# VectorE's C product between the next slot's two scans, B products two slots ahead, column border at 384

## Chip, cores and metric

The kernel runs on one core of a Trainium2 chip. The metric is the time of one execution on the device in microseconds (us). The time before the change is the median of four runs.

## What is computed

Two residual blocks on x of shape (4, 512, 64, 64), float32: 4 batches, 512 channels, 4096 tokens.

```python
# layer 0: group norm, layer norm, a selective state-space model on each quarter of the channels
xn = layer_norm(tokens(group_norm(x)))
for each of 4 chunks of 128 channels:
    xi, z = split(chunk @ in_proj.T)               # 256 inner channels
    xc = silu(causal_conv4(xi) + conv_b)
    dt, Bs, Cs = split(xc @ x_proj.T)              # 8 + 16 + 16 columns
    dt = softplus(dt @ dt_proj.T + dt_b)
    # for every inner channel d and state s, over the tokens in order:
    h = exp(dt * A) * h + (dt * xc) * Bs
    y = sum_s(h * Cs) + xc * D
    chunk = (y * silu(z)) @ out_proj.T + skip * chunk
x = x + layer_norm(chunks) @ proj.T + proj_b
# layer 1: group norm, linear attention with relu on q and k, output projection, residual
x = x + attention(group_norm(x))
```

## The kernel before

The tokens of a batch are cut into tiles of T = 512. A **step** is one batch, one tile and one chunk of 128 channels: 4 x 8 x 4 = 128 steps. The recurrence over tokens is done by VectorE's scan instruction, which computes a * h + b along the 512 tokens for 128 partitions. A partition holds one pair of state and channel: 32 channels times 4 states. A step has 256 inner channels and 16 states, that is 32 scans, in 16 **slots** of two scans. In a step the slots go over e (two halves of the inner channels), q (four groups of four states) and jj (two pairs of channel blocks). Two slots, an even and an odd one, share one tile h and one C tile.

For slot g the engines do this:

- SyncE loads `b_all` (`b_row`): four rows of B, each spread over 32 partitions, for two slots at once, and `d_all` (`spread`): dt and dt * xc, twice a step. There are three buffers of `b_all` and two of `d_all`.
- GpSimd (POOL) makes the **B product** `bx` (`drive`, L467): 128 x 1024 elements. It is emitted one slot ahead, with two buffers.
- ScalarE (ACT) makes `dA` = exp(dt * A) into a PSUM bank (`decay`, L459), one for each scan, two scans ahead; there are two banks.
- VectorE (DVE) does the two scans (L484) and then the **C product** (L493), in place: h times C on the columns up to `CUT`, with C read from PSUM.
- The columns from `CUT` to 512 are the **border**: POOL multiplies them for both slots of a pair (L500) after the odd slot, with a copy of C that ScalarE makes (`c_copy`, L451). `CUT` is 512 - 160 = 352. Ahead of it POOL saves the last column of h as the state for the next tile (L499).
- TensorE (PE) spreads C over the partitions with a matmul (`c_row`, tile `c_all`, one PSUM bank) and sums h over the states into `y` (`fold_states`, 4 matmuls) after the odd slot.

All engines work through their queues in the order in which the program emits, which is written out by hand (`manual_schedule`). After the scans and the product of a slot `after()` emits the other work, by the slot number s in the step: at s = 1 the transfer of `d_all` for the second half, the `gate` product on POOL (L528) and the time-step matmuls; at s = 2 a table load, two softplus and another table load on ScalarE, and the output projection; at s = 3 the time-step product on POOL (L386) and its store; at s = 3 to 7 the input projection and convolution of a later step (`inputs`: matmuls `pc` and `pz`, copies `xz`, L359 and L368); at s = 9 another gate and `spread`; at s = 10 silu between two table loads, and the skip; from s = 11 the matmuls `pd` and the copies that make `dtr` and the parts of C (`mixers`).

The rest of the two layers lies in lists of pieces, `late` (layer norms, projection) and `rest` (attention). A credit of 3.2 matmuls a slot decides how many pieces a slot takes; slots 2 and 10 take none from there but one piece that may hold a long VectorE operation ("wide", 128 x 2048 elements).

The product and the C copy wait for each other in a chain: the even slot's product, the C copy, the odd slot's product.

Of the kernel before, what the change touches and what calls it, by code (L numbers as in the profile page):

```python
# [8 lines left out]
F32 = mybir.dt.float32  # L9
BF16 = mybir.dt.bfloat16  # L10
# [4 lines left out]
P = 128  # L15
T = 512
# [8 lines left out]
def kernel(  # L25
# [29 lines left out]
    NH = DI // P  # L55
    SUB = T // P
    LANE = 32
    CUT = T - 160
    BLK = 32
    KS = P // BLK  # L60
    NQ = NST // KS
# [59 lines left out]
        )  # L121
    sel = sel.rearrange("p q k i -> p q (k i)")

    minus = []
    for i in (2, 3):
        m = const.tile([P, P], BF16, tag=f"minus{i}", name=f"minus{i}")
        nc.vector.memset(m, 0.0)
        nc.vector.tensor_scalar(m[i * LANE :, :], ident[i * LANE :, :], -1.0, None, ALU.mult)
        minus.append(m)

    fold = const.tile([P, BLK], F32, tag="fold", name="fold")
    for k in range(KS):
# [19 lines left out]


    w_cv = const.tile([P, NTAP, DI], F32, tag="w_cv", name="w_cv")
    w_x = wk.tile([P, DI], F32, tag="bx", name="w_x", bufs=2)
    nc.scalar.dma_start(w_x, in_w[:, 0:DI])
    conv_bc = wk.tile([P, NTAP, DI], F32, tag="h", name="conv_bc", bufs=2)
    nc.scalar.dma_start(conv_bc, conv_w.partition_broadcast(P))
# [31 lines left out]
    w_qk = const_rows(wqk, "w_qk")  # L190

    bqk = const.tile([P, 2 * C], BF16, tag="bqk", name="bqk")
    b_all = wk.tile([P, 2 * C], F32, tag="bx", name="b_all", bufs=2)
    nc.scalar.dma_start(b_all, b_qkv[0 : 2 * C].partition_broadcast(P))
    bv = column(b_qkv[2 * C : 3 * C], NC, "bv")
    bo = column(b_out, NC, "bo")
# [177 lines left out]
            mm(f["pt"][e], w_dt[:, e * P : (e + 1) * P], f["dtr"][0:RANK, :], start=True, stop=True)  # L374

    def time_steps(f, nm):
        both = f["both"] = wk.tile([P, 2, NH, T], F32, tag="dt", name=f"dt_{nm}", bufs=1)
        for e in range(NH):
            nc.scalar.activation(
                both[:, 0, e, :], f["pt"][e], AF.Softplus, bias=dtb[:, e : e + 1]  # L380
            )

    def to_rows(f, v, nm):
# [16 lines left out]
    def mixers(f, nm):  # L400

        pd = work_bank(f"pd_{nm}")
        for e in range(NH):
            mm(pd, w_xp[:, e, :], f["xz"][:, 0, e, :], start=(e == 0), stop=(e == NH - 1))
        yield
        dtr = f["dtr"] = wk.tile([RANK + NST, T], F32, tag="dtr", name=f"dtr_{nm}", bufs=1)
        nc.scalar.copy(dtr, pd[0 : RANK + NST, :])
        b_rows = f["b_rows"] = dram.tile([NST, T], F32, tag="b_rows", name=f"b_rows_{nm}", bufs=3)  # L410
        nc.sync.dma_start(b_rows, dtr[RANK:, :])
        parts = f["parts"] = wk.tile([P, T], BF16, tag="parts", name=f"parts_{nm}", bufs=3)
        nc.scalar.copy(parts, pd)
        for i in (2, 3):
            yield
            mm(pd, minus[i - 2], parts, start=False, stop=True, skip_group_check=True)
            yield
            nc.scalar.copy(parts[i * LANE :, :], pd[i * LANE :, :])

# [1 line left out]

    JJ = NJ // 2
    SLOTS = NH * NQ * JJ

    def place(g):

# [36 lines left out]
    def drive(g):  # L463

        n, e, q, jj = place(g)
        bxs[g] = wk.tile([P, 2, T], F32, tag="bx", name=f"bx_{g}", bufs=2)
        nc.gpsimd.tensor_tensor(  # L467
            bxs[g], fs[n]["d_all", e][:, 1, jj * 2 : jj * 2 + 2, :], bc(b_all[g // JJ], 2), ALU.mult
        )

    def slot(g, last, in_scan, after):
        n, e, q, jj = place(g)
        b, t, c = steps[n]
        if jj and g + 5 < last:
            b_row(g + 5)
        if g + 1 < last:
            drive(g + 1)
        if jj == 0:
            hs[g // JJ] = wk.tile([P, NJ, T], F32, tag="h", name=f"h_{g}", bufs=2)
        h = hs[g // JJ]  # L480
        own = h[:, jj * 2 : jj * 2 + 2, :]
        for i in range(2):
            j = jj * 2 + i
            nc.vector.tensor_tensor_scan(  # L484
                h[:, j, :], dAs.pop(2 * g + i), bxs[g][:, i, :],
                0.0 if t == 0 else st[:, c, e, q, j : j + 1], ALU.mult, ALU.add,
            )
            if 2 * g + i + LEAD < 2 * last:
                decay(2 * g + i + LEAD)
        del bxs[g]  # L490
        in_scan()

        nc.vector.tensor_tensor(  # L493
            own[:, :, :CUT], own[:, :, :CUT], bc(c_all[g // JJ][:, :CUT], 2), ALU.mult
        )
        if jj == 0:
            c_copy(g)
        if jj == JJ - 1:
            nc.gpsimd.tensor_copy(st[:, c, e, q, :], h[:, :, T - 1])  # L499
            nc.gpsimd.tensor_tensor(  # L500
                h[:, :, CUT:], h[:, :, CUT:], bc(c_sb.pop(g // JJ), NJ), ALU.mult
            )
            if g + 1 < last:
                c_row(g + 1)
            fold_states(g)
        after()

    def fold_states(g):

# [243 lines left out]
    for g in range(0, 3 * JJ, JJ):  # L753
        b_row(g)
    c_row(0)
    drive(0)
    for k in range(LEAD):
        decay(k)

    with tc.manual_schedule():  # L760
        credit, mix = 0.0, iter(())
        for n, (b, t, c) in enumerate(steps):
            f, nm = fs[n], names[n]
            before = fs[n - 1] if n else None
            nxt = fs[n + 1] if n + 1 < N else None
            front = step_inputs(n + 2) if n + 2 < N else iter(())
            last_mix, mix = mix, mixers(fs[n + 2], names[n + 2]) if n + 2 < N else iter(())
            if c == 0 and (t + 1 < NT or b + 1 < B):
                add_to(late, tile_norm(b, t + 1) if t + 1 < NT else tile_norm(b + 1, 0))
            if c == 0 and t == 0 and b + 1 < B:  # L770
                add_to(light, input_norm(b + 1))
            if c == 2:
                while late and (b, t + 1) in xn and late[0][0].__name__ == "tile_norm":
                    one(late)
            for s in range(SLOTS):
                def in_scan():
                    if s == 0 and before is not None:
                        take_y(before, n - 1, 1)
                    if s == SLOTS // 2:
                        take_y(f, n, 0)  # L780

                def after():
                    nonlocal credit
                    start = work["mm"]
                    if s == 1:
                        spread(f, 1, nm)
                        if before is not None:
                            gate(before, 1)
                        if nxt is not None:
                            time_banks(nxt, names[n + 1])  # L790
                    if s == 2:
                        if nxt is not None:
                            nc.scalar.preload_act_table_set("softplus")
                            time_steps(nxt, names[n + 1])
                            nc.scalar.preload_act_table_set("natural_log_exp_and_others")
                        if before is not None:
                            out_proj(before, names[n - 1])
                    if s == 0:
                        next(last_mix, None)
                    if s == 10 and before is not None:  # L800
                        pb_, pt_, pc_ = steps[n - 1]
                        with_skip(before, xn[pb_, pt_], pc_)
                        if pc_ == NC - 1:
                            add_to(late, leave(pb_, pt_))
                    if s == 3:
# [12 lines left out]
                    if s >= 11:  # L818
                        next(mix, None)
                    if s in (2, 10):  # L820
                        if not (late and late[0][1] and one(late)):
                            one(light)
                        credit = 0.0
                        return
                    credit = min(credit + 3.2 - (work["mm"] - start), 3.2)
                    for queue in (late, rest):
                        if credit > 0:
                            start = work["mm"]
                            one(queue, wide=False)
                            credit -= work["mm"] - start  # L830

                slot(n * SLOTS + s, N * SLOTS, in_scan, after)
            fs[n - 1].clear() if n else None
    take_y(fs[N - 1], N - 1, 1)
    gate(fs[N - 1], 1)
    out_proj(fs[N - 1], names[N - 1])
# [57 lines left out]
```

## Time and profile before

| | |
|---|---|
| time, median of 4 runs | 8965.38 us (8948.59 to 8980.93) |
| profiled execution | 8961.52 us, span 8959.8 us |
| mean granted clock of TensorE | 0.863 |
| VectorE, GpSimd, TensorE, ScalarE busy | 7456.6, 7152.1, 6931.0, 5522.2 us |
| one scan; one C product; one B product; one border product; one dA | 1267, 888, 2359, 1541, 687 ns |
| first and last C product | 126.7 and 8465.7 us after the start |

The slots lie between these last two times; ahead of them the constants and the first statistics are made, and behind them the last batch's attention is finished. A line of the groups view gives the source line, the engine, the operation, the tiles it writes and reads with their shapes, the count, then the busy time in us with the mean duration of one in ns, then how long the engine sat idle before these instructions and what ended most of that. In the timeline the first column is the start in us, the second the duration of what was merged, and the bracket tells the idle time ahead and who ended it.

### The profile page before, as it was taken

Reading aid. Unit: us, or ns where it says so; the run is one execution under the profiler, and the core shown is the slowest. Engines: PE = TensorE matmul, PEld = TensorE weight load, DVE = VectorE, ACT = ScalarE, POOL = GpSimd, SP = SyncE. Lnnn points to the kernel's source line nnn. Section 1 sums busy time; section 2 is a strip of 40 time slices with the busy share of each in tenths; the row PEclk is TensorE's granted clock in tenths of the full one; section 3 lists DMA queues with packets and bytes.
Section 4 is the critical chain, followed back from the end, with each engine's and each line's share of the span. In section 5 each row is a group of like instructions: output and inputs, shape, how many; then the busy total and the mean of one; then the engine's idle time right before and its main releaser. Section 6 shows DMA issues by size and latency. Waiting matters only on the chain.

```text
span 8959.8 us, 80504 instructions
## 1 busy us (share of the span) xinstructions
PE 6931.0 (77%) x20885; PEld 2443.6 (27%) x20960; DVE 7456.6 (83%) x7097; ACT 5522.2 (62%) x8480; POOL 7152.1 (80%) x4565
## 2 busy tenths in 40 slices
PE   4667667677788877788788878778878887788799
PEld 1122222122223222232223222222222332222244
DVE  5998998888988888888888988888888888888700
ACT  4666666666666666666666666666666666666421
POOL 4988888888888888888888888888888888888600
PEclk8777787777889888899888989989888988989899
DMA  5555555555555555556554555556555555555502
GB/s 145 142 131 138 126 138 127 125 130 136 138 134 136 130 137 139 133 156 158 150 134 126 150 133 140 131 138 167 144 132 140 127 128 131 132 136 152 139 33 84
DMA packets 628274, 1197.31 MB, mean 134 GB/s; under 512 B 116056, under 2 KB 116576, under 8 KB 615520
## 3 DMA queue, kind: packets, MB, share of 16 engines
q1 hardware_dynamic: 620928, 1187.44, 51.8%
q10 hardware_dynamic: 6880, 4.70, 0.2%
q8 instruction: 164, 2.69, 0.1%
q14 instruction: 302, 2.47, 0.1%
HBM read 986.17 MB, written 205.52 MB: 133 GB/s over the span
## 4 chain that ended last, share of the span: by engine, by line
POOL 31%; PE 19%; issue 15%; DVE 15%; DMA 11%; ACT 5%; SPq 4%; POOLq 0%; DVEq 0%; ACTq 0%
POOL bx L467 23%; DVE h L484 12%; DMA d_all<-d_rows 7%; PE y L84 4%; PE pq L84 3%; PE pd L84 3%; PE pr L84 3%; POOL h L500 3%; POOL dt L386 2%; SPq L397 2%; PE pc L84 2%; DMA b_all<-b_rows 2%; POOL xz L528 2%; DVE h L493 2%; SPq L437 1%
## 5 line engine op out<-in xcount | busy, mean ns | idle before, releaser
L467 POOL TENSOR_TENSOR bx<-d_all,b_all 128x1024 f32<-128x1024 f32 x2048 | 4794.9, 2359 | 202.4 <-DVE h L484 184.9
L484 DVE TENSOR_TENSOR_SCAN h<-dA,st,bx 128x512 f32<-128x512 f32 x3584 | 4394.2, 1267 | 523.0 <-ACT dA L459 291.3
L459 ACT ACTIVATE dA<-d_all,a_t 128x512 f32<-128x512 f32 x4096 | 2771.3, 687 | 1781.4 <-DVE h L484 1770.5
L493 DVE TENSOR_TENSOR h<-h,c_all 128x704 f32<-128x704 f32 x2048 | 1818.9, 888 | 274.2 <-PE c_all L84 56.5
L84 PE MATMUL c_all<-parts,sel 128*128 128x512 bf16 x1024 | 448.0, 437 | 1592.0 <-DVE h L493 1589.2
L500 POOL TENSOR_TENSOR h<-h,c_sb 128x640 f32<-128x640 f32 x1024 | 1577.9, 1541 | 83.2 <-POOL st L499 1.8
L84 PE MATMUL y<-h,fold 128*32 128x512 f32 x8192 | 1360.8, 743 | 221.1 <-POOL h L500 218.5
L84 PE MATMUL pq<-w_qk,xa 128*128 128x512 f32 x2048 | 979.2, 611 | 6.3 <-issue 3.8
L84 PE MATMUL pc<-xn,w_cv 128*128 128x512 f32 x2048 | 946.1, 616 | 4.6 <-ACT xn L298 4.6
L499 POOL COPY st<-h 128x4 f32<-128x4 f32 x1024 | 191.8, 187 | 902.3 <-DVE h L484 862.2
L84 PEld LDWEIGHTS y<-h,fold 128*32 128x32 f32 x8192 | 175.4, 118 | 2172.2 <-POOL h L500 1880.3
L484 DVE TENSOR_TENSOR_SCAN h<-dA,bx 128x512 f32<-128x512 f32 x512 | 597.0, 1207 | 129.1 <-POOL bx L467 78.9
L84 PE MATMUL pr<-xb,m 128*128 128x512 f32 x1024 | 513.8, 645 | 66.8 <-DMA xb<-x 66.8
L84 PEld LDWEIGHTS pc<-xn,w_cv 128*128 128x128 f32 x2048 | 390.1, 196 | 582.8 <-issue 530.7
L84 PEld LDWEIGHTS pq<-w_qk,xa 128*128 128x128 f32 x2048 | 403.0, 198 | 448.1 <-issue 434.3
L84 PE MATMUL pp<-xn,w_pr 128*128 128x512 f32 x1024 | 484.6, 604 | 5.0 <-DVE xn L294 4.2
L451 ACT COPY c_sb<-c_all 128x160 f32<-128x160 f32 x1024 | 298.1, 291 | 260.8 <-DVE h L493 258.2
L359 ACT ACTIVATE xz<-pc,cb 128x512 f32<-128x512 f32 x256 | 175.9, 687 | 423.1 <-PE pc L84 389.0
L84 PE MATMUL pd<-xz,w_xp 128*128 128x512 f32 x512 | 395.9, 917 | 0.0
L84 PEld LDWEIGHTS <-sel 128*128 128x128 bf16 x1280 | 128.2, 100 | 973.6 <-DVE h L493 676.8
L561 DVE TENSOR_TENSOR kq<-pk,kq 128x512 f32<-128x512 f32 x124 | 85.1, 687 | 312.8 <-PE pk L84 312.5
L84 PE MATMUL y<-xz,dg 128*128 128x512 f32 x512 | 339.3, 752 | 0.0
(137 smaller groups left out, 7078.0 us busy)
## 6 DMA issues: line engine op xcount, KB each, us to landing
d_all<-d_rows SPq DMA_DIRECT2D x2048, 256.0 KB, 6.6
b_all<-b_rows SPq DMA_DIRECT2D x4096, 64.0 KB, 2.1
d_rows<-dt SPq DMA_DIRECT2D x256, 512.0 KB, 4.0
xs<-in_x_dram SPq DMA_DIRECT2D x32, 1024.0 KB, 11.3
xn<-in_x_dram SPq DMA_DIRECT2D x32, 1024.0 KB, 5.4
xr<-in_x_dram SPq DMA_DIRECT2D x32, 1024.0 KB, 5.4
x<-xr SPq DMA_DIRECT2D x32, 1024.0 KB, 3.9
xa<-x SPq DMA_DIRECT2D x32, 1024.0 KB, 5.4
```

The source lines that it names most:

```text
L84: nc.tensor.matmul(out_, lhsT, rhs, **how)
L359: nc.scalar.activation(xz[:, 0, e, :], pc[e], AF.Identity, bias=cb[:, e : e + 1])
L386: nc.gpsimd.tensor_tensor(f["both"][:, 1], f["both"][:, 0], f["xz"][:, 0], ALU.mult)
L397: nc.sync.dma_start(d[k * BLK : (k + 1) * BLK, v], src)
L451: nc.scalar.copy(got, c_all[g // JJ][:, CUT:])
L459: nc.scalar.activation(dAs[k], fs[n]["d_all", e][:, 0, j, :], AF.Exp, scale=a_t[:, e, j, q : q + 1])
L467: nc.gpsimd.tensor_tensor(bxs[g], fs[n]["d_all", e][:, 1, jj * 2 : jj * 2 + 2, :], bc(b_all[g // JJ], 2), ALU.mult)
L484: nc.vector.tensor_tensor_scan(h[:, j, :], dAs.pop(2 * g + i), bxs[g][:, i, :], 0.0 if t == 0 else st[:, c, e, q, j : j + 1], ALU.mult, AL ...
L493: nc.vector.tensor_tensor(own[:, :, :CUT], own[:, :, :CUT], bc(c_all[g // JJ][:, :CUT], 2), ALU.mult)
L499: nc.gpsimd.tensor_copy(st[:, c, e, q, :], h[:, :, T - 1])
L500: nc.gpsimd.tensor_tensor(h[:, :, CUT:], h[:, :, CUT:], bc(c_sb.pop(g // JJ), NJ), ALU.mult)
L528: nc.gpsimd.tensor_tensor(f["xz"][:, 1, e, :], f["xz"][:, 1, e, :], f["y", e], ALU.mult)
```

## The change

- The C product of slot g is emitted between the two scans of slot g + 1, with the C copy behind it and, for an odd slot, the next `c_row` and the fold. Slots 3 and 11 of a step (`BEHIND`) are the exception: their product comes after their own two scans. The border product stays at the end of the odd slot.
- `drive` is emitted two slots ahead, and `bx` has three buffers. `b_row` moves from odd slots (five ahead) to even slots (six ahead).
- `CUT` is 384 in place of 352: VectorE's product gets 2 x 384 elements a partition, POOL's border 4 x 128.
- What makes room for the third buffer: one matrix `minus` in place of two, and `dtr` as a part of the tile `dt` (`both`), which is now allocated in `mixers`.
- `take_y` moves from ahead of the product to the beginning of `after()`.

```diff
-    CUT = T - 160
+    CUT = T - T // 4
...
-        bxs[g] = wk.tile([P, 2, T], F32, tag="bx", name=f"bx_{g}", bufs=2)
+        bxs[g] = wk.tile([P, 2, T], F32, tag="bx", name=f"bx_{g}", bufs=3)
...
+    AWAY = (2, 10)
+    BEHIND = [s + 1 for s in AWAY]
...
-    def slot(g, last, in_scan, after):
+    def slot(g, last, after):
         n, e, q, jj = place(g)
         b, t, c = steps[n]
-        if jj and g + 5 < last:
-            b_row(g + 5)
-        if g + 1 < last:
-            drive(g + 1)
+        if g + 2 < last:
+            drive(g + 2)
         if jj == 0:
+            if g + 3 * JJ < last:
+                b_row(g + 3 * JJ)
             hs[g // JJ] = wk.tile([P, NJ, T], F32, tag="h", name=f"h_{g}", bufs=2)
...
             if 2 * g + i + LEAD < 2 * last:
                 decay(2 * g + i + LEAD)
+            if i == 0 and g and (g - 1) % SLOTS not in BEHIND:
+                product(g - 1, last)
         del bxs[g]
-        in_scan()
-
-        nc.vector.tensor_tensor(
-            own[:, :, :CUT], own[:, :, :CUT], bc(c_all[g // JJ][:, :CUT], 2), ALU.mult
-        )
-        if jj == 0:
-            c_copy(g)
         if jj == JJ - 1:
             nc.gpsimd.tensor_copy(st[:, c, e, q, :], h[:, :, T - 1])
             nc.gpsimd.tensor_tensor(
                 h[:, :, CUT:], h[:, :, CUT:], bc(c_sb.pop(g // JJ), NJ), ALU.mult
             )
+        if g % SLOTS in BEHIND:
+            product(g, last)
+        after()
+
+    def product(g, last):
+        _, _, _, jj = place(g)
+        own = hs[g // JJ][:, jj * 2 : jj * 2 + 2, :CUT]
+        nc.vector.tensor_tensor(own, own, bc(c_all[g // JJ][:, :CUT], 2), ALU.mult)
+        if jj == 0:
+            c_copy(g)
+        if jj == JJ - 1:
             if g + 1 < last:
                 c_row(g + 1)
             fold_states(g)
-        after()
...
-        dtr = f["dtr"] = wk.tile([RANK + NST, T], F32, tag="dtr", name=f"dtr_{nm}", bufs=1)
+        f["both"] = wk.tile([P, 2, NH, T], F32, tag="dt", name=f"dt_{nm}", bufs=1)
+        dtr = f["dtr"] = f["both"][0 : RANK + NST, 1, NH - 1, :]
...
-            mm(pd, minus[i - 2], parts, start=False, stop=True, skip_group_check=True)
+            mm(pd, minus, parts, start=False, stop=True, skip_group_check=True)
```

More of the change, by code (lines that the diff above doesn't have):

```diff
@@ L122 @@
     sel = sel.rearrange("p q k i -> p q (k i)")
[L124 to L129, printed above, removed]
+    minus = const.tile([P, P], BF16, tag="minus", name="minus")
+    nc.vector.memset(minus, 0.0)
+    nc.vector.tensor_scalar(minus[2 * LANE :, :], ident[2 * LANE :, :], -1.0, None, ALU.mult)
     fold = const.tile([P, BLK], F32, tag="fold", name="fold")
@@ L154 @@
     w_cv = const.tile([P, NTAP, DI], F32, tag="w_cv", name="w_cv")
-    w_x = wk.tile([P, DI], F32, tag="bx", name="w_x", bufs=2)
+    w_x = wk.tile([P, DI], F32, tag="bx", name="w_x", bufs=3)
     nc.scalar.dma_start(w_x, in_w[:, 0:DI])
@@ L192 @@
     bqk = const.tile([P, 2 * C], BF16, tag="bqk", name="bqk")
-    b_all = wk.tile([P, 2 * C], F32, tag="bx", name="b_all", bufs=2)
+    b_all = wk.tile([P, 2 * C], F32, tag="bx", name="b_all", bufs=3)
     nc.scalar.dma_start(b_all, b_qkv[0 : 2 * C].partition_broadcast(P))
@@ L376, in time_steps @@
     def time_steps(f, nm):
-        both = f["both"] = wk.tile([P, 2, NH, T], F32, tag="dt", name=f"dt_{nm}", bufs=1)
         for e in range(NH):
             nc.scalar.activation(
-                both[:, 0, e, :], f["pt"][e], AF.Softplus, bias=dtb[:, e : e + 1]
+                f["both"][:, 0, e, :], f["pt"][e], AF.Softplus, bias=dtb[:, e : e + 1]
             )
@@ L469, in drive @@
         )
-    def slot(g, last, in_scan, after):
+    def slot(g, last, after):
         n, e, q, jj = place(g)
         b, t, c = steps[n]
-        if jj and g + 5 < last:
-            b_row(g + 5)
-        if g + 1 < last:
-            drive(g + 1)
+        if g + 2 < last:
+            drive(g + 2)
         if jj == 0:
+            if g + 3 * JJ < last:
+                b_row(g + 3 * JJ)
             hs[g // JJ] = wk.tile([P, NJ, T], F32, tag="h", name=f"h_{g}", bufs=2)
         h = hs[g // JJ]
-        own = h[:, jj * 2 : jj * 2 + 2, :]
         for i in range(2):
@@ L755 @@
     c_row(0)
-    drive(0)
+    for g in range(2):
+        drive(g)
     for k in range(LEAD):
@@ L775, with after @@
             for s in range(SLOTS):
-                def in_scan():
+                def after():
+                    nonlocal credit
+                    start = work["mm"]
                     if s == 0 and before is not None:
@@ L780, in in_scan @@
                         take_y(f, n, 0)
-                def after():
-                    nonlocal credit
-                    start = work["mm"]
                     if s == 1:
@@ L819, in after @@
                         next(mix, None)
-                    if s in (2, 10):
+                    if s in AWAY:
                         if not (late and late[0][1] and one(late)):
@@ L830, in after @@
                             credit -= work["mm"] - start
-                slot(n * SLOTS + s, N * SLOTS, in_scan, after)
+                slot(n * SLOTS + s, N * SLOTS, after)
             fs[n - 1].clear() if n else None
+        product(N * SLOTS - 1, N * SLOTS)
     take_y(fs[N - 1], N - 1, 1)
```

## The prediction

> **What bounds the kernel now.** I read the page's busy shares and cost groups first, then the waits, then the timeline of one stretch in the middle. The groups show what a slot is made of and what its engines idle for:
>
> ```profile
> PE 6931.0 (77%) x20885; PEld 2443.6 (27%) x20960; DVE 7456.6 (83%) x7097; ACT 5522.2 (62%) x8480; POOL 7152.1 (80%) x4565
> ...
> L467 POOL TENSOR_TENSOR bx<-d_all,b_all 128x1024 f32<-128x1024 f32 x2048 | 4794.9, 2359 | 202.4 <-DVE h L484 184.9
> L484 DVE TENSOR_TENSOR_SCAN h<-dA,st,bx 128x512 f32<-128x512 f32 x3584 | 4394.2, 1267 | 523.0 <-ACT dA L459 291.3
> L459 ACT ACTIVATE dA<-d_all,a_t 128x512 f32<-128x512 f32 x4096 | 2771.3, 687 | 1781.4 <-DVE h L484 1770.5
> L493 DVE TENSOR_TENSOR h<-h,c_all 128x704 f32<-128x704 f32 x2048 | 1818.9, 888 | 274.2 <-PE c_all L84 56.5
> ...
> L500 POOL TENSOR_TENSOR h<-h,c_sb 128x640 f32<-128x640 f32 x1024 | 1577.9, 1541 | 83.2 <-POOL st L499 1.8
> ```
>
> No engine is full: DVE 83%, POOL 80%. There are 2048 slots in 128 steps of 16, some 65 us a step. DVE idles mostly in front of scans, and the waits view names two causes of about equal size:
>
> ```profile
> DVE h L484 <- ACT dA L459: 337.2, 256, 4.9
> ...
> DVE h L484 <- POOL bx L467: 278.3, 181, 46.5
> ...
> ACT c_sb L451 <- DVE h L493: 258.2, 649, 4.9
> ```
>
> (us in total, times, longest; 46.5 of the bx wait is the start of the kernel.) The change can take away the bx wait only; the dA wait comes from ScalarE, which stands in its queue behind table loads and behind copies that wait for TensorE. The third line: the C copy runs only after the product that reads the same C tile. The timeline of slots 2 to 5 of one step shows how these hang together:
>
> ```profile
> 4002.70 2.45 DVE L484 TENSOR_TENSOR_SCAN h<-dA,st,bx 128x512 f32<-128x512 f32 x2
> ...
> 4005.25 0.89 DVE L493 TENSOR_TENSOR h<-h,c_all 128x704 f32<-128x704 f32 x1
> ...
> 4006.23 0.29 ACT L451 COPY c_sb<-c_all 128x160 f32<-128x160 f32 x1 [0.35 <-DVE h L493]
> 4006.54 1.28 ACT L793 ACT_TABLE_LOAD   x1
> ...
> 4007.28 2.46 DVE L484 TENSOR_TENSOR_SCAN h<-dA,st,bx 128x512 f32<-128x512 f32 x2 [1.14 <-POOL bx L467]
> ...
> 4007.83 1.26 ACT L379 ACTIVATE dt<-pt,dtb 128x512 f32<-128x512 f32 x2
> ...
> 4010.07 1.53 POOL L500 TENSOR_TENSOR h<-h,c_sb 128x640 f32<-128x640 f32 x1
> ...
> 4011.19 2.46 DVE L484 TENSOR_TENSOR_SCAN h<-dA,st,bx 128x512 f32<-128x512 f32 x2 [0.46 <-PE c_all L84]
> 4011.57 2.35 POOL L386 TENSOR_TENSOR dt<-dt,xz 128x1024 f32<-128x1024 f32 x1
> ...
> 4013.89 4.65 POOL L467 TENSOR_TENSOR bx<-d_all,b_all 128x1024 f32<-128x1024 f32 x2
> ...
> 4016.27 2.46 DVE L484 TENSOR_TENSOR_SCAN h<-dA,st,bx 128x512 f32<-128x512 f32 x2 [1.63 <-POOL bx L467]
> 4016.45 0.69 ACT L359 ACTIVATE xz<-pc,cb 128x512 f32<-128x512 f32 x1 [1.43 <-PE pc L84]
> ```
>
> Slot 5's scans (4016.27) wait 1.63 us for a B product that POOL could begin only after the border product (L500) and the time-step product (L386). Slot 4's scans start when dA is ready, behind two table loads. And the copy at 4016.45 waits for TensorE's pc, which was queued behind the fold that waits for L500.
>
> **The change, part by part.** A step is 65.1 us; all sums are for one step, times 127.
>
> *The product between two scans.* Two scans in a row take 2.45 us although one takes 1.267: the second starts 0.08 before the first ends. The product starts 0.10 after the scan whose result it reads (4002.70 + 2.45 = 4005.15, then 4005.25). So that dependence costs 0.18 us. Between scans of another slot it should go: 14 of 16 slots (slots 3 and 11 keep the old place), 14 x 0.18 = 2.5 us. In the Trainium skill, "VectorE: DVE Perf Modes", section "The DRAIN you can't avoid", says that leaving out a semaphore between VectorE operations saves nothing, the next one waits for the pipe in any case; by that this term would be 0, and my forecast would rise by about 80 us to no change. The two intervals above, -0.08 and +0.10, disagree with it, and I go by them.
>
> *The border at 384.* Each VectorE product grows from 704 to 768 elements a partition. From 888 ns at 704 and 2280 ns at 2048 (L294) a further element costs 1.036 ns: +66 ns, 16 x 0.066 = +1.06 us. POOL's border product falls from 640 elements (1541 ns) to 512; the gate L528 of 512 elements takes 1274 ns: 8 x 0.267 = -2.1 us on POOL. The C copy on ScalarE falls from 0.29 to about 0.27.
>
> *B products two slots ahead.* The third buffer lets POOL write slot g+2's product as soon as slot g-1's scans are done, a slot (3.3 us) before it is needed in time. The 1.63 us of slot 5 and the like go, 278.3 - 46.5 = 232 us in all, 1.8 us a step. What is late next? In slot 4 dA, unchanged. In slots 6 and 7 dA again: in its queue stand the two copies of pc. I counted this over steps 2 to 125 of the timeline, from the end of slot 2's scans: slot 7's first dA ends at 18.9 us on average, and its scan starts at 19.4. So slot 7 already starts on ScalarE's word, and most of the bx wait is hidden by that. SP: the four b_row DMAs of a pair move from an odd slot, five ahead, to the even slot, six ahead; they and their reader both move by one, the lead stays four slots (14 us) against 2.1 us to landing. The d_all transfer is needed one slot (about 4 us) earlier; its last part is issued some 19 us before its first reader now and lands in 6.6 (longest 12.1). Both cost nothing; without that cover a B product would stall by what is missing.
>
> *What the later product does to others.* The product is emitted one scan later, and with it the C copy, the C broadcast and the fold. On ScalarE the C copy of slots 2 and 10 now stands behind the table loads and the dA of slots 4 and 12. Counted from the end of slot 2's scans: dA 0.74, load, two softplus and load 3.85 (1.28 + 1.26 + 1.28 and gaps), dA 0.69, copy 0.27: 5.6 us; behind silu likewise 0.74 + 1.28 + 1.91 + 1.28 + 0.69 + 0.27 = 6.2. The border product of slots 3 and 11 waits for it, and so does the odd product. It ends at 5.6 + 1.27 = 6.9 (7.1 now, on average) and 7.5 (7.5 now): the shorter border pays for the later start, no more. Behind it stand, on TensorE, fold and pc (slot 3) or fold and pd (slot 11), then ScalarE's copies, then slot 7's and slot 14's dA.
>
> So at slots 7 and 14 the scan starts at dA's time, and one product (0.87 us) is still to be done that is done by then now:
> - Slots 3 to 7: the fold follows the border at once in the new order (it starts 1.0 us after it now, TensorE being busy); I take half of that. dA at 18.4, slot 8 at 18.45 + 3.26 = 21.7, with the product 22.6, against 22.9 now: -0.3.
> - Slots 8 to 10: order gained and border paid, net 0.11 a slot: -0.2.
> - Slots 11 to 14: now the scan starts at 15.9 from the end of slot 10's scans, dA being ready at 15.1; new 15.3 + 0.87: +0.35.
> - Slots 14 to 2: four to five products at 0.11: -0.45.
>
> Sum -0.6 us a step, 127 x 0.6 = 76 us. The profiled execution took 8961.5 us (span 8959.8), the median of the runs is 3.9 above: 8885 and 8890.
>
> *Edits of no price.* One minus matrix instead of two (the second pass also subtracts in rows nobody reads): same matmuls, 0.2 us at the start. dtr inside the dt tile: its copy may wait for the d_rows DMAs of slot 3, nine slots earlier; without that cover it would wait the 4.0 us they take. take_y moves behind the product and waits for a fold emitted in its own slot; ScalarE has about 1.3 us to spare there, beyond that slot 2 or 10 waits for dA.
>
> **The rivals.**
> *All of it counts*: 2.5 - 1.06 + 1.8 = 3.2 us a step, 410 us: about 8560. For it: bx and the order are both on VectorE's path, and POOL has least to spare in steps without other work. Against: slot 7's dA follows at once. Chance 0.17.
> *TensorE late with C*: the broadcast and the fold now stand behind the work given out at the end of the slot before. From slot 3 to slot 6 TensorE does two pc groups (3.7 + 3.4 us), pz and perhaps two matmuls more, 0.9 to 2.6 us more than now before that broadcast. TensorE idles 1589 us in front of c_all now, which speaks against it. If the products of slots 6 and 14 wait 0.6 us a step together, nothing is left: 8960. Chance 0.13.
> *Slower*: the C copy behind the table loads delays border, fold, pc and pd, so that the dA of slots 7 and 14 comes no earlier than now. Then the uncovered product is paid in full at both, 2 x 0.87 = 1.74, less 0.65 from the order in the other slots: +1.1 us a step, 140 us: 9105. It decides from the point where the folds of slots 3 and 11 start no earlier than 8.1 and 7.6 us after the scans of slots 2 and 10, which are today's averages. For it: with nothing else on VectorE in slot 10 the border is 0.9 us later than today. Chance 0.27.
>
> **How the numbers follow.** My forecast has 0.43, with 8800 to 8950 of its own. What can be told from no change here is 0.3%, 27 us. Faster: 0.43 and 0.17, less a little: 0.59. Same: 0.13. Slower: 0.28. The range leaves out the ends of the first and third rival: 8640 to 9100.
>
> **What would show it.** Right: products start 0.08 before the scan ahead ends; bx waits under 60 us; dA waits above 337; border of slot 3 starting right after the C copy. The dA waits at slots 7 and 14 falling, or waits of products for c_all above 150 us, would prove the sum wrong.

## The result, and the profile after

| | before | after |
|---|---|---|
| time, median of 63 and of 42 runs | 8965.79 us | 8978.36 us (8962.81 to 8987.05) |
| profiled execution's span | 8959.8 us | 8976.8 us |
| mean granted clock of TensorE | 0.863 | 0.865 |

The ratio is 1.0012, interval 1.0008 to 1.0017: 0.12% slower, which is inside the bound of 0.3% named in the prediction. The forecast was 0.8% faster.

The page of the changed kernel, busy shares and cost groups (the columns as in the page before):

```profile
PE 6905.8 (77%) x20882; PEld 2443.7 (27%) x20960; DVE 7413.2 (83%) x7095; ACT 5422.8 (60%) x8480; POOL 6856.4 (76%) x4565
...
L482 DVE TENSOR_TENSOR_SCAN h<-dA,st,bx 128x512 f32<-128x512 f32 x3584 | 4469.4, 1270 | 496.9 <-issue 249.9
L466 POOL TENSOR_TENSOR bx<-d_all,b_all 128x1024 f32<-128x1024 f32 x2048 | 4790.8, 2359 | 99.8 <-DVE h L482 84.9
...
L505 DVE TENSOR_TENSOR h<-h,c_all 128x768 f32<-128x768 f32 x2048 | 1906.5, 931 | 359.7 <-ACT c_sb L450 235.3
...
L493 POOL TENSOR_TENSOR h<-h,c_sb 128x512 f32<-128x512 f32 x1024 | 1298.3, 1268 | 546.1 <-issue 223.8
...
L356 ACT ACTIVATE xz<-pc,cb 128x512 f32<-128x512 f32 x256 | 175.9, 687 | 529.4 <-PE pc L84 529.4
```

GpSimd got its room: 6856 us busy against 7152, and its B products idle 100 us where they idled 202. VectorE kept its idle time: 497 us ahead of these scans where it was 523, and 360 ahead of products where it was 274. New is what the products wait for: the C copy (`c_sb`). And ScalarE's `xz` copies wait 529 us for `pc` on TensorE, 389.0 before.

What VectorE gained and lost between its first scan and its last product can be added up from the two traces. A gap is the time from the end of one VectorE instruction to the start of the next; it is negative where the next one starts early. The gaps under 0.2 us ahead of products went from +209 to -122 us in all: so 331 us were gained. The larger products take 87 us more, and the gaps over 0.2 us, in which VectorE waits for another engine, grew from 741 to 983 us. With some 20 us more at the scans nothing is left.

The waits of the changed kernel (us in total, times, longest):

```profile
PE c_all L84 <- DVE h L505: 1697.6, 630, 15.6
PEld y L84 <- POOL h L493: 1363.0, 344, 8.6
...
ACT xz L356 <- PE pc L84: 529.4, 255, 4.9
...
DVE h L482 <- issue: 302.5, 198, 5.5
...
DVE h L505 <- ACT c_sb L450: 235.3, 139, 2.4
...
DVE h L482 <- ACT dA L458: 141.1, 106, 4.4
...
DVE h L505 <- PE c_all L84: 107.0, 46, 7.7
```

The scans' waits for `bx` fell from 278.3 to 54.0 us, of which 46.2 are the start of the kernel. The lines "issue" and "dA" of the scans have to be read with care, because a scan's wait is booked under the semaphore that came last by the profile. I went through every scan that started later than the instruction ahead of it allowed, and put the delay to whichever of its `dA` and `bx` had ended last. By slot, in us over the whole run (the last two rows are experiments, told below):

| | bx, slots 3 / 5 / 11 | dA, slot 4 | 6 | 7 | 12 | 14 |
|---|---|---|---|---|---|---|
| before | 39 / 177 / 20 | 114 | 42 | 45 | 37 | 123 |
| after | none | none | 220 | 126 | none | 193 |
| `e10_late_no_exception` | none | 108 | none | 86 | 80 | 26 |
| `e11_fold_behind` | 44 / 162 / 21 | 90 | none | 4 | 36 | 6 |

So the `bx` waits went, and the `dA` waits of slots 6, 7 and 14 took their place. Why `dA` is late there is seen in the timeline of slots 2 to 5 of one step of the changed kernel (start, duration, engine, idle time ahead and who ended it); slot 2's scans end at 3989.8:

```profile
3990.55 1.28 ACT L797 ACT_TABLE_LOAD   x1
3990.89 0.93 DVE L505 TENSOR_TENSOR h<-h,c_all 128x768 f32<-128x768 f32 x1
3991.74 1.28 DVE L482 TENSOR_TENSOR_SCAN h<-dA,st,bx 128x512 f32<-128x512 f32 x1
...
3995.05 0.26 ACT L450 COPY c_sb<-c_all 128x128 f32<-128x128 f32 x1
...
3995.34 0.95 DVE L505 TENSOR_TENSOR h<-h,c_all 128x768 f32<-128x768 f32 x1 [2.32 <-ACT c_sb L450]
3995.45 1.26 POOL L493 TENSOR_TENSOR h<-h,c_sb 128x512 f32<-128x512 f32 x1 [1.34 <-DMA d_all<-d_rows]
...
3996.35 0.38 PE L84 MATMUL c_all<-parts,sel 128*128 128x512 bf16 x1 [3.07 <-DVE h L505]
...
3996.77 1.22 PE L84 MATMUL y<-h,fold 128*32 128x512 f32 x8
3997.92 8.63 PE L84 MATMUL pc<-xn,w_cv 128*128 128x512 f32 x16
```

Slot 2's product is done at 3991.8, but its C copy comes only at 3995.05, behind the table loads. Slot 3's product, one of the two that stayed behind their own scans, waits 2.32 us for that copy with VectorE idle. The border reads the copy too and starts 0.14 us behind it (the bracket names a DMA, the one that landed last by the profile). On TensorE the broadcast of the next C (`c_all`) waits 3.07 us for slot 3's product, the fold behind it for the border, and `pc` stands behind both: it starts 8.1 us after slot 2's scans.

Over steps 2 to 125 a step takes 65.33 us, before 65.35: in the middle of the kernel nothing changed. The 17 us between the two profiled executions lie at the ends. The first scan starts 3.4 us later, steps 0 and 1 (up to the end of slot 2's scans in step 2) take 7.2 more, the 120 us from the end of slot 2's scans in step 126 to the end of the last product contain 11.8 more (there three products wait 4.88, 5.39 and 3.92 us for `c_all`, where the longest such wait before was 1.38), and 124 steps together with the tail give 5.3 back.

### The profile page after: what moved, and what is told of

It is laid out like the page before. It is cut to its first block, busy times and chain, and to the rows that moved or that the text cites. A ratio compares the mean times of both kernels' runs of the same rounds, so it can differ in the third digit from the quotient of the medians.

```text
span 8976.8 us, 80691 instructions
## 1 busy us (share of the span) xinstructions
PE 6905.8 (77%) x20882; PEld 2443.7 (27%) x20960; DVE 7413.2 (83%) x7095; ACT 5422.8 (60%) x8480; POOL 6856.4 (76%) x4565
## 5 line engine op out<-in xcount | busy, mean ns | idle before, releaser
L482 DVE TENSOR_TENSOR_SCAN h<-dA,st,bx 128x512 f32<-128x512 f32 x3584 | 4469.4, 1270 | 496.9 <-issue 249.9
L458 ACT ACTIVATE dA<-d_all,a_t 128x512 f32<-128x512 f32 x4096 | 2815.4, 689 | 1938.6 <-DVE h L482 1917.2
L505 DVE TENSOR_TENSOR h<-h,c_all 128x768 f32<-128x768 f32 x2048 | 1906.5, 931 | 359.7 <-ACT c_sb L450 235.3
L493 POOL TENSOR_TENSOR h<-h,c_sb 128x512 f32<-128x512 f32 x1024 | 1298.3, 1268 | 546.1 <-issue 223.8
L84 PE MATMUL pt<-dt,w_dt 8*128 8x512 f32 x512 | 350.4, 815 | 4.0 <-ACT dt L406 2.7
```

Of the source, the lines that this page charges most:

```text
L84: nc.tensor.matmul(out_, lhsT, rhs, **how)
L458: nc.scalar.activation(dAs[k], fs[n]["d_all", e][:, 0, j, :], AF.Exp, scale=a_t[:, e, j, q : q + 1])
L482: nc.vector.tensor_tensor_scan(h[:, j, :], dAs.pop(2 * g + i), bxs[g][:, i, :], 0.0 if t == 0 else st[:, c, e, q, j : j + 1], ALU.mult, AL ...
L493: nc.gpsimd.tensor_tensor(h[:, :, CUT:], h[:, :, CUT:], bc(c_sb.pop(g // JJ), NJ), ALU.mult)
L505: nc.vector.tensor_tensor(own, own, bc(c_all[g // JJ][:, :CUT], 2), ALU.mult)
```

## Experiments

All ratios are against runs of the kernel before that were taken together with those of the experiment; their medians lie between 8966 and 8974 us, so differences of less than 10 us between two experiments mean little. At first three theories stood against one another for the lost gain: the late C copy of slots 2 and 10; the `dA` waits that take the place of the `bx` waits, whatever the copy does; and TensorE coming late with the broadcast of C. Later runs tested a fourth, the exception itself, that is the slots 3 and 11 in which the product, the `c_row` and the fold stay ahead of the other work.

### The parts alone

**The border alone** (`e4_cut_only`): before, with one line changed.

```diff
-    CUT = T - 160
+    CUT = T - T // 4
```

> The kernel before with the border at 384. VectorE's product grows by some 43 ns (931 against 888 ns as measured in the changed kernel), 88 us in all; POOL's border falls from 1541 to 1268 ns, which brings the B products of slots 3, 5 and 11 forward by 0.27 us, some 50 to 80 us. All theories: 8940 to 9010 us; this prices the border alone.

8951.35 us, 0.9976 (0.9967 to 0.9984): a gain of 21 us, and not a loss, though VectorE is the busiest engine.

```profile
L493 DVE TENSOR_TENSOR h<-h,c_all 128x768 f32<-128x768 f32 x2048 | 1955.4, 955 | 272.7 <-PE c_all L84 55.2
```

The C product takes 955 ns here, 67 more than the 888 of before. The 931 ns of the changed kernel, from which the expectation took its 43, hold a second thing: at its later place a product is shorter by some 25 ns whatever the border (888 ns at the old place and 861 in `e13_late_352` with the border at 352; 955 and 929 in `e10_late_no_exception` with 384). So 2 x 67 ns of VectorE were worth less here than GpSimd's 270 ns a border. TensorE's granted clock was higher as well (0.872 in the median of these runs, 0.861 in those of the kernel before), and its share of the 21 us isn't known.

**B products two slots ahead, alone** (`e2_ahead_only`): before, with the three buffers and what makes room for them.

```diff
-        if jj and g + 5 < last:
-            b_row(g + 5)
-        if g + 1 < last:
-            drive(g + 1)
+        if g + 2 < last:
+            drive(g + 2)
...
+            if g + 3 * JJ < last:
+                b_row(g + 3 * JJ)
```

> The kernel before, with nothing but the B products two slots ahead in three buffers (and the room for it: one minus matrix, dtr inside dt, b_row at even slots); product order and border at 352 stay. Both theories: the bx wait falls from 278 to about 50 us. Copy theory: the C copy keeps its early place, so most of the 232 us are gained: 8760 to 8850 us. dA theory: the waits turn into dA waits of slots 6 and 7 one for one: 8930 to 8965 us.

8934.75 us, 0.9956 (0.9943 to 0.9970): a gain of 37 us of the 232 that the scans' waits for `bx` amounted to. The waits turned into `dA` waits: by the same count as above 161 us in slot 4, 118 in slot 6, 99 in slot 7, 122 in slot 14.

**The later product alone** (`e3_order_only`): the changed kernel with `drive` one slot ahead, two buffers and the border at 352.

> The changed kernel with B products one slot ahead in two buffers again and the border at 352: the product's place is all that is left. The order saves 0.18 us in 14 slots of a step. Copy theory: border and odd product wait for the late C copy, the B product of slot 5 comes still later behind the border, so the bx wait rises above 350 us and the time to 9000 to 9100 us. dA theory: the product that is still open when dA comes late costs about what the order saves: 8940 to 8990 us.

9404.56 us, 1.0483 (1.0469 to 1.0497), far beyond both expectations. The waits view of this kernel tells why:

```profile
DVE h L482 <- POOL bx L466: 1078.0, 710, 48.3
```

With two buffers the B product of slot g + 1 can start when the scans of slot g - 1 are done, and is needed by the first scan of slot g + 1. Between them VectorE used to do product, scan, scan, product, about 4.3 us. In the new order it does scan, product, scan, about 3.3 us. Behind an odd slot GpSimd needs 1.55 + 0.19 + 2.36 = 4.1 us for border, state and B product. The waits for `bx` indeed lie in the odd slots alone, 63 to 403 us in each. So the later product needs the third buffer: the two parts are not independent, and their prices alone don't add up.

**B products ahead and border, product at its old place** (`e9_no_order`): `e2_ahead_only` with `CUT` at 384.

> B products two slots ahead and the border at 384, with the product directly behind its own two scans as before (the C copy then stands ahead of the table loads by itself). Copy theory with the parts adding: e2 (8935) less what the border alone gave (21): about 8910, so the product's new place is worth 130 us once the C copy is early. If the product's place is worth its full 0.18 us in 14 slots (320 us): 9100 would be needed, which nothing supports. If it is worth nothing: 8780.

8910.71 us, 0.9934 (0.9920 to 0.9949), as expected. With two of the three parts the kernel is 55 us faster than before; with the third it is 13 us slower.

### The C copy

**Late copy in the kernel before** (`e6_copy_late`): the C copy of slots 2 and 10 moves behind the table loads, all else stays.

```diff
+            if i == 0 and (g - 1) % SLOTS in (2, 10):
+                c_copy(g - 1)
...
-        if jj == 0:
+        if jj == 0 and g % SLOTS not in (2, 10):
             c_copy(g)
```

> The kernel before, with one thing changed: the C copy of slots 2 and 10 is emitted in the next slot behind its first scan and dA, and so behind the table loads, where the change has put it. Copy theory: the border products of slots 3 and 11 and the odd product wait for the copy as in the changed kernel (products wait some 200 us for it), the B product of slot 5 comes later behind the border: 100 to 250 us slower than before, 9070 to 9220 us. dA theory: within 40 us of before.

9126.34 us, 1.0176 (1.0158 to 1.0193). The late copy by itself costs 160 us, 1.3 a step.

**Early copy in the changed kernel** (`e1_copy_first`): the C copy of slots 2 and 10 is emitted right after their scans, ahead of the table loads.

```diff
+        if g % SLOTS in AWAY:
+            c_copy(g)
...
-        if jj == 0:
+        if jj == 0 and g % SLOTS not in AWAY:
             c_copy(g)
```

> The changed kernel, with the C copy of slots 2 and 10 emitted right after the slot's scans, ahead of the table loads, and the product of these slots after it. Copy theory (the C copy behind the table loads holds the border product, the odd product, and so the fold and pc or pd, and gives the gains back): products no longer wait for the C copy (235 us now), the border product of slot 3 starts 1 to 2 us earlier where no long VectorE operation stands in slot 2, dA waits of slots 6, 7 and 14 shrink; 8750 to 8880 us against 8978. dA theory (ScalarE's queue and TensorE's pc and pd set the dA of slots 6, 7 and 14 whatever the C copy does): dA waits there stay above 450 us in all, and the time within 30 us of 8978. TensorE theory (broadcast and fold come late behind the work handed out before): no change either, and products still wait for c_all over 100 us.

8779.49 us, 0.9785 (0.9772 to 0.9798): the late copy costs the changed kernel 199 us. But the `dA` waits did not go away: 145, 126 and 190 us in slots 6, 7 and 14. The products wait 89 us for `c_all`, under the 100 that the TensorE theory needed.

**The `xz` copies one slot later** (`e7_xz_later`): `e1_copy_first`, with the four copies of `pc` and `pz` to `xz` emitted a slot later, so that `dA` doesn't stand behind a copy that waits for TensorE.

> The changed kernel with the early C copy (8779 us), and the four copies xz emitted one slot later than now, so that each comes two slots behind its matmuls. dA theory, in the part that is left to it: the dA waits of slots 6 and 7 (270 us together in that kernel) are ScalarE waiting for pc ahead of dA; they fall below 80 us, the wait of xz for pc from 452 to under 100 us, and the time by 60 to 200 us, to 8580 to 8720. If the dA is late for another reason (VectorE itself frees the bank late), the waits stay and the time is within 30 us of 8779.

8760.16 us, 0.9768 (0.9752 to 0.9784). The `dA` waits of slots 6 and 7 fell from 270 to 40 us, but the time fell by 19 us only, against 60 to 200 expected: from slot 2 to slot 8 a step is 0.97 us shorter, from slot 8 to slot 10 it is 0.76 longer, and the products' waits for `c_all` rose from 89 to 224 us. So the order of ScalarE's queue is not what costs the time. That `pc` comes late on TensorE is what is left, and the next experiments test it.

### The exception

**No exception, early copy** (`e8_no_exception`) and **no exception, late copy** (`e10_late_no_exception`): one line of `e1_copy_first` and the same line of the changed kernel.

```diff
-    BEHIND = [s + 1 for s in AWAY]
+    BEHIND = []
```

> The changed kernel with the early C copy, and slots 3 and 11 no longer excepted: all products between the next slot's scans. The broadcast and fold of slot 3 then stand behind pc on TensorE. dA theory: pc no longer waits for the border and the fold, so the dA waits of slots 6 and 7 fall below 150 us (270 now); against it the products of slots 4 and 5 wait for c_all. TensorE theory: those waits are larger, over 200 us: 8800 to 8950 us. If the first weighs more: 8650 to 8750.

> The changed kernel with one thing altered: slots 3 and 11 are no longer excepted; the C copy of slots 2 and 10 stays late, behind the table loads. If the exception cost what it did with the early copy (8779 to 8442, 337 us) and the late copy costs its 199 us besides: 8640. If the late copy hurts only through the exception (there the odd product follows at once and waits for it, and the fold and pc behind that): 8440 to 8500, and products wait for the C copy less than 60 us.

8441.88 us, 0.9410 (0.9394 to 0.9426), and 8404.14 us, 0.9364 (0.9351 to 0.9377). Both are below everything that was expected (8650 and 8440 at the lowest). So that one line costs the changed kernel 574 us, and without it the late copy does no harm: the kernel with it is 38 us the faster. The page and the waits of `e10_late_no_exception`:

```profile
PE 6784.8 (81%) x20882; PEld 2422.0 (29%) x20960; DVE 7380.5 (88%) x7095; ACT 5418.7 (64%) x8480; POOL 6848.0 (82%) x4565
```

```profile
PE c_all L84 <- DVE h L505: 908.7, 500, 15.9
PEld y L84 <- POOL h L493: 678.9, 352, 6.4
...
DVE h L482 <- ACT dA L458: 155.2, 120, 4.2
...
DVE h L505 <- PE c_all L84: 109.0, 43, 8.0
ACT xz L356 <- PE pc L84: 93.3, 85, 3.4
...
```

The work is the same, the shares rise. TensorE waits 909 us for a product ahead of the broadcast of C where it waited 1698 in the changed kernel, its folds wait 679 us for a border where they waited 1363, and ScalarE's `xz` copies wait 93 us for `pc` where they waited 529. The same slots in the timeline of this kernel; slot 2's scans end at 3732.8:

```profile
3736.44 3.60 PE L84 MATMUL pc<-xn,w_cv 128*128 128x512 f32 x8
3738.09 0.26 ACT L450 COPY c_sb<-c_all 128x128 f32<-128x128 f32 x1
3738.24 1.28 DVE L482 TENSOR_TENSOR_SCAN h<-dA,st,bx 128x512 f32<-128x512 f32 x1 [2.18 <-issue]
3738.49 1.27 POOL L493 TENSOR_TENSOR h<-h,c_sb 128x512 f32<-128x512 f32 x1 [1.39 <-ACT c_sb L450]
3739.44 0.93 DVE L505 TENSOR_TENSOR h<-h,c_all 128x768 f32<-128x768 f32 x1
...
3740.73 1.06 PE L84 MATMUL y<-h,fold 128*32 128x512 f32 x8
3741.73 3.70 PE L84 MATMUL pc<-xn,w_cv 128*128 128x512 f32 x8
```

The C copy is as late as in the changed kernel, 5.3 us after slot 2's scans. But slot 3's product is now done in slot 4, when the copy is there, and the first `pc` group runs at 3.6 us, ahead of the broadcast and the fold, while TensorE would otherwise wait for the product and the border. On average over steps 2 to 125 the first `pc` matmul starts 4.8 us after slot 2's scans, 8.6 in the changed kernel, and the first `pd` matmul 4.1 us after slot 10's, 9.7 in the changed kernel.

The mean time from mark to mark over steps 2 to 125, in us, cuts the step into four parts. "s8" is the start of slot 8's first scan, "2 end" the end of slot 2's scans; where one product is still to be done at a mark, 0.85 has been added to the part before it and taken from the part behind:

| | 2 end to s8 | s8 to 10 end | 10 end to s14 | s14 to 2 end | step |
|---|---|---|---|---|---|
| before | 22.88 | 9.69 | 15.87 | 16.92 | 65.35 |
| after | 22.66 | 9.55 | 16.59 | 16.52 | 65.33 |
| `e10_late_no_exception` | 20.39 | 9.55 | 14.29 | 16.54 | 60.77 |

The exception costs 2.27 and 2.30 us a step, in the parts that hold slots 3 and 11, and nothing in the two others. How much of it is the product that waits for the copy, and how much the place of the broadcast and of the fold, was not tried in the changed kernel one by one.

**The fold behind the other work, in the kernel before** (`e11_fold_behind`): the products stay at their old place; in slots 3 and 11 only the other work is emitted ahead of `c_row` and the fold, so that `pc` and `pd` stand before them in TensorE's queue.

```diff
+            if g % SLOTS in (3, 11):
+                after()
             if g + 1 < last:
                 c_row(g + 1)
             fold_states(g)
+            if g % SLOTS in (3, 11):
+                return
         after()
```

> The kernel before, with one thing moved: in slots 3 and 11 the broadcast of the next C and the fold are emitted behind the work of the slot, so that on TensorE pc and pd stand ahead of them. Queue-order theory (pc and pd wait in TensorE's queue behind a fold that waits for POOL's border): the dA wait of slot 14 (about 129 us) goes nearly, that of slots 6 and 7 shrinks, the B product of slot 5 still comes late behind the border (175 us stay): 8800 to 8900 us against 8966. If the fold's place does not matter: 8940 to 8990. If the broadcast coming later holds the products: over 9000 us, and products wait for c_all above 150 us.

8858.47 us, 0.9872 (0.9858 to 0.9885). The `dA` waits of slots 6, 7 and 14 all but vanish (table above), while the `bx` wait of slot 5 stays. The products wait more for the broadcast, which comes later: 56.5 us before, 215 now, without the loss that the last expectation tied to it.

```profile
DVE h L484 <- POOL bx L467: 257.1, 174, 46.9
...
DVE h L493 <- PE c_all L84: 215.4, 169, 6.6
```

**The same with B products ahead and the border at 384** (`e14_ahead_fold_behind`): `e9_no_order` with the edit of `e11_fold_behind`.

> B products two slots ahead and the border at 384 with the product directly behind its own scans (8911 us), and in slots 3 and 11 the broadcast and the fold behind the work of the slot. What is left against the changed kernel without the exception (8404) is the product's place. If the place is worth its 0.18 us in all 16 slots, 127 x 2.9 = 366 us: about 8770. If most of the gain is the fold's place and the B products' lead: 8450 to 8600. If the products wait for c_all in slots 4 and 12 as they did with the fold behind in the kernel before (215 us): about 8900.

8789.10 us, 0.9795 (0.9782 to 0.9809). Against `e9_no_order` the place of the broadcast and the fold is worth 122 us; against `e10_late_no_exception`, in which the products also lie between the next slot's scans, 385 us are left. That is 385 / (127 x 16) = 0.19 us a product. The profiled executions, 416 us apart (411 of them between the first scan and the last product), show what it is made of, by the same count of gaps as for the changed kernel: 361 us are short gaps ahead of products, 0.18 us each. The shorter products (52 us) and the waits over 0.2 us (503 against 460) add 95, and the scans take 47 back.

### A faster version

With the fold out of the way, VectorE and not GpSimd should set the time, so I put the border back to 352, in `e8_no_exception` (`e12_border_352`) and in `e10_late_no_exception` (`e13_late_352`).

> The fastest kernel so far (early C copy, no exception, 8442 us) with the border back at 352. VectorE is 88% busy there, GpSimd 81%. If VectorE sets the time: 43 ns less in 2048 products, 60 to 90 us faster, 8350 to 8385. If GpSimd's longer border (273 ns in 1024 products) delays the B products or the fold: 8440 to 8520, and the scans wait for bx above 80 us.

> The changed kernel without the exception (8404 us), with the border at 352. VectorE's products are 43 ns shorter, GpSimd's border 273 ns longer. If VectorE sets the time as with the early C copy, where this gave 45 us: 8350 to 8375. If the border, which waits for the late C copy here, is what the fold waits for: 8400 to 8450.

8397.16 us, 0.9357 (0.9345 to 0.9370), and 8375.14 us, 0.9335 (0.9323 to 0.9348): 45 and 29 us less than with 384. `e13_late_352` is the fastest kernel of the study: the change with `BEHIND` empty and the border left where it was. Both expectations counted 43 ns a product; it is 68 to 70, some 140 us in all, of which only 45 and 29 came through. The rest went into longer waits: VectorE's gaps over 0.2 us grew from 476 to 594 us and from 460 to 527. So VectorE alone doesn't set the time here either.

## Why the prediction was wrong

**Right: the product between two scans.** The median product starts 81 ns before the scan ahead of it ends; at the old place it starts 104 ns after it. The forecast's 0.18 us a product is what the short gaps give between `e14_ahead_fold_behind` and `e10_late_no_exception`; that their times give 0.19 is in part luck, since other terms nearly cancel there.

The Trainium skill, "VectorE: DVE Perf Modes", section "The DRAIN you can't avoid", says that dropping a semaphore between two VectorE operations saves nothing, which would have put this at 0; the gaps of -81 and +104 ns and the 385 us show that it doesn't carry over to an operation that reads the result of the one ahead. (No run here drops a semaphore; the change puts another operation between the two.) The prediction said that a price of 0 would raise the forecast by about 80 us to no change. By its own terms it is more: the sum counts the 0.18 us in two slots from 8 to 10 and in four to five from 14 to 2, some 1.2 us a step or 150 us. The unchanged time of the changed kernel thus speaks for neither price and has another cause. The same section adds that a next operation that isn't held starts earlier, and the -81 ns agrees with that.

**Right, with small misses: the prices of single steps.** The C product at 384 takes 955 ns at the old place (`e4_cut_only`), where 954 were estimated; in the changed kernel it takes 931, because the later place makes it shorter, which the prediction didn't have. The border takes 1268 instead of 1274, the C copy comes 5.8 and 6.2 us after the scans of slots 2 and 10 (5.6 and 6.2 forecast), and the `bx` wait is gone and has turned into waits for `dA`.

**The sum by parts of the step.** "Slots 3 to 7", forecast -0.3, measured -0.22. "Slots 8 to 10", forecast -0.2, measured -0.14. "Slots 14 to 2", forecast -0.45, measured -0.40. "Slots 11 to 14", forecast +0.35, measured +0.72. This last term is the step that failed. (Its own numbers, 15.3 + 0.87 against 15.9, give +0.27 and not +0.35, so the miss is a little larger still.) I let slot 14's first scan start when its `dA` is ready, at 15.3 us from the end of slot 10's scans. `dA` is ready at 15.17, but the scan starts at 15.74. In a third of the steps (42 of 124, against 62 before) it starts over 0.2 us later than `dA` allows, by 1.5 us on average. In 24 of the 42 the statistics of the residual (`xr`) stand in VectorE's queue right ahead of that scan, in 6 pieces of the attention (`kq`), and in 12 the scan ahead ends late itself. The gap of 0.8 us between `dA` and scan stood in the trace of before and I wrote it down; I took it to vanish, and 0.57 of it stayed. The four parts give -0.04 (the two steps of the table -0.02) where I had -0.6, and 0.37 of the difference is this one term; the other three missed by 0.05 to 0.08 each, all to the same side. These are means of one execution of each kernel, and no experiment took the VectorE work out of slot 14.

**Not in the sum: the ends.** I multiplied a middle step by 127 and so put the ends at no change. The first and the last steps and the start add 22.4 us, the opposite sign to the middle.

**Not seen: what the exception costs.** I treated slots 3 and 11 as two slots in which the 0.18 us is not gained. In fact there the product waits 235.3 us for the late C copy in all, 121.9 in slot 3 and 126.9 in slot 11 by my count of all delays. And there the broadcast of the next C, which waits for that product, and the fold, which waits for the border, stand ahead of `pc` and `pd` in TensorE's queue. The prediction named that queue ("the copy at 4016.45 waits for TensorE's pc, which was queued behind the fold that waits for L500"), but priced only how much earlier the fold starts, and not what its place costs. The exception as a whole, product, broadcast and fold, costs 574 us: without it the kernel goes beyond the rival "all of it counts" (8560), to 8404.

**The rivals.** *TensorE late with C* is out for the middle of the kernel: the products' waits for `c_all` are 107 us in all, below the 150 named, and of these about 14 each fall to slots 6 and 14. *Slower* has its mechanism shown and its bound half met. The late copy costs 199 us in the changed kernel and 160 in the one before. Slot 3's fold starts 7.4 us after slot 2's scans, earlier than the bound of 8.1, and slot 11's starts 7.8 after slot 10's, later than its 7.6. Accordingly the first half of the step gained and the part behind slot 11 lost, and the sum came to nothing.

**The tests I had named.** Products starting 0.08 early, `bx` waits under 60 and the border right behind the C copy came true. So did `dA` waits above 337, but only by the count of delays (539 in slots 6, 7 and 14, and 34 in slots 2 and 3); the line of the waits view that the 337 came from fell to 141.1, the rest being booked under "issue" and other names. The time was wrong all the same. These tests were of the mechanisms, and none of them of the one term that decided most between -0.6 and 0.

## What to carry to other kernels

In an in-order queue, ask of every instruction that waits what stands behind it and needn't wait: a broadcast of 0.4 us and a fold of 1.1 us that waited for VectorE and GpSimd held back the matmuls of a later step. That cost about 120 us by itself, and 574 us together with the product tied to it. When a change moves a step "everywhere except in two slots", price the exception by itself, with everything emitted beside it. And when a trace shows a gap between the last input and the start of an instruction, find out what fills it before letting it vanish in a sum.

## What the runs showed that I had not expected

- Parts don't add. Alone, the B products ahead bring -37 us and the border -21, and the later product costs 432; all three together with the exception cost 13, and without it bring -570.
- TensorE's granted clock is not the same in all kernels: 0.865 in the changed one at 77% busy, 0.885 without the exception at 81%, but 0.884 in `e11_fold_behind` at 78%. What raises it was not tried, nor how much of the gains it is. TensorE's busy time fell by 121 of the 574 us in the first case, and in `e11_fold_behind` by 69 of the 116 that it gained.
- A C product that lies between two scans is itself shorter: 929 ns where it takes 955 behind its own scans. 64 more elements a partition cost 67 ns at the old place and 68 at the new one, as the mean rate up to 2048 elements had it (66).
- A later copy was better than an early one once nothing waited for it: 8404 against 8442 us.
